# The query and output-weight products of an attention layer, made in two column halves of the array

## The chip, the cores and the metric

The kernel runs on one core of one Trainium2 chip. The metric is device time in microseconds (us) of one execution; three executions of the kernel before gave 2745.74, 2745.95 and 2746.96 us, and the median, 2745.95 us, is the time before.

## The reference

Four graph layers run over 4096 nodes with 256 features. Each ends in a residual sum and a row normalization. Layer 0 is the one that the change touches; layer 1 is a graph attention, layers 2 and 3 are products with the normalized adjacency matrix.

```
qkv = x @ Wqkv + bqkv                       # x: 4096 x 256, q, k, v: 256 wide each, 4 heads of 64
scores = einsum('hnd,hmd->hnm', q, k) * 64 ** -0.5
scores = scores + graph_bias * adj
scores = where(adj == 0, -1e9, scores)
attn = softmax(scores)
out = einsum('hnm,hmd->hnd', attn, v)       # heads side by side: 4096 x 256
x = layernorm(x + out @ Wout + bout)
```

Everything is in float32.

## The kernel before, in words

**Tiling of layer 0.** The 4096 rows are taken in 32 blocks of 128 (`Rows`, one for each block `ib`). A block has two pairs of heads (`Pair`, `pr` 0 and 1), and each pair goes through the 4096 columns in four steps of 1024. So one block is eight steps, and layer 0 is 256 steps, numbered `t`, with a tail of eight more. The keys (`kT`, in the tensor `store`) and the values (`v_sb`, in the tensor `xc`) stay on chip.

**A step.** `step(t)` writes the order of the work out by hand, under a manual schedule, as a software pipeline. On PE the order in a step is: `score` of the newest step (line 371), the transposes of the exponentials of head 0 of an older step (`turn`, line 410), `attend` of a step older still (line 428), then `finish` or `begin` if one is due, then the transposes of head 1 (line 410 again). ACT takes the exponentials (line 396), copies the transposed tiles out of PSUM (line 418) and makes the 0/1 edge mask with its row sums (line 295). DVE adds the bias and takes the maximum (line 380), makes the bias of the next block (lines 278, 283, 284) and does the small work of a pair. No planner is involved: what stands earlier in `step` is issued earlier on its engine.

**Which part of the array each product uses.** The page's forms tell it, as rows times columns:

- `score`: 64*128. Two heads of 64 features each stand in the two row halves.
- `turn`: 64*128. The two row halves of a tile are transposed by two instructions.
- `attend`: 128*64. `v_sb[:, ci, h * HD : (h + 1) * HD]` of one head (64 columns) is the stationary operand, and the head `j` of the pair writes the partitions `j * HD` to `(j + 1) * HD` of `po`. So the two heads stand in the two column halves.
- `begin` (query product, line 319) and `finish` (output-weight product, line 340): 128*128, the whole array.

A float32 product of the program appears as two MATMUL records with a weight load (LDWEIGHTS) each; a transpose appears as one. `attend` has 16 products and 32 records in a step, `begin` 4 products and 8 records, `finish` 2 products and 4 records.

**begin.** `Rows.begin` (lines 314 to 335) makes the queries of the next block from `wq_sb` and `self.xq` into the PSUM tile `pq`, in one bank of the two that `po` alternates between; DVE adds the query bias, scales, and writes `qT` (line 327). It is called once for a block, in its sixth step, right after `attend` and ahead of the second `turn`. The first two blocks are different: `begin` of block 0 lies in the preamble between two key projections (line 212), and that of block 1 lies between two `turn`s, because no `attend` runs yet.

**finish.** `Rows.finish` (lines 337 to 353) multiplies the scaled heads `oT` with `wout_sb` into the PSUM tile `pp`; DVE adds the residual (line 350), takes the statistics for the normalization (lines 115, 116), and SP writes the row block to DRAM. It is called once for a block, in the eighth step, right after `attend` and ahead of the second `turn`. The last one runs in the tail, after the product of line 609 and ahead of line 139.

Of the kernel before, what the change touches and what calls it, by code (L numbers as in the profile page):

```python
# [16 lines left out]
P = 128  # L17
N = 4096
D = 256
H = 4  # L20
HD = D // H
# [23 lines left out]
def tile_gnn(  # L45
# [18 lines left out]
    nc = tc.nc  # L64
# [48 lines left out]
    def ln_stats(pool, row, ci):  # L113
        st = pool.tile([P, 6], F32, tag="bnst", name="bnst")
        nc.vector.bn_stats(st, row)
        nc.vector.bn_aggr(mv[:, ci, :], st)
# [54 lines left out]
    with ExitStack() as l0:  # L171
# [16 lines left out]
        wq_sb = w_sb[:, :, 0:D]  # L188
# [3 lines left out]
        wout_sb = big.tile([P, 2, D], F32, name="wout_sb")  # L192
# [55 lines left out]
        class Rows:  # L248
# [65 lines left out]
            def begin(self, tag):  # L314
                self.qT = wk2.tile([P, 2, P], F32, tag="qT", name="qT")
                pq = ps_o.tile([P, 512], F32, tag=tag, name="pq")
                for pr in range(2):
                    for cc in range(2):
                        nc.tensor.matmul(  # L319
                            pq[:, pr * P : (pr + 1) * P],  # L320
                            wq_sb[:, cc, pr * P : (pr + 1) * P],
                            self.xq[:, cc, :],
                            start=(cc == 0),
                            stop=(cc == 1),
                        )
                for pr in range(2):
                    nc.vector.tensor_scalar(
                        self.qT[:, pr, :],
                        pq[:, pr * P : (pr + 1) * P],
                        bqk_sb[:, pr : pr + 1],  # L330
                        HD ** -0.5,
                        ALU.add,
                        ALU.mult,
                    )
                nc.gpsimd.tensor_tensor(self.xr, self.xr, bout_b, ALU.add)

            def finish(self, tag):
                pp = ps_o.tile([P, 512], F32, tag=tag, name="pp")
                for pr in range(2):
                    nc.tensor.matmul(  # L340
                        pp[:, 0:D],
                        self.oT[:, pr, :],
                        wout_sb[:, pr, :],
                        start=(pr == 0),
                        stop=(pr == 1),
                    )
                nc.vector.tensor_reduce(
                    rowsum[:, self.ib : self.ib + 1], self.rs, AX.X, ALU.add
                )
                nc.vector.tensor_tensor(self.xr, pp[:, 0:D], self.xr, ALU.add)  # L350
                ln_stats(wk2, self.xr, self.ib)
                if self.ib + 1 < NCH:
                    nc.sync.dma_start(x0_pre[self.ib * P : (self.ib + 1) * P, :], self.xr)
# [798 lines left out]
```

## Time and profile before

| what | value |
|---|---|
| median of three executions | 2745.95 us |
| profiled execution, its own time | 2743.03 us |
| profiled execution, span from the first to the last instruction | 2741.3 us |
| mean granted TensorE clock of the span | 0.993 |
| PE busy | 2688.6 us, 98% of the span |
| DVE busy | 2183.8 us, 80% |
| ACT busy | 1648.0 us, 60% |
| layer 0, first score to last score | about 20 us to 1355 us |

How to read it. PE is TensorE's matmuls, PEld its weight loads, DVE is VectorE, ACT is ScalarE, POOL is GpSimd, SP issues transfers. A matmul's record begins when it starts and ends when its last result is out, so records overlap; the distance between two starts tells what an instruction costs in a full stream, and its own duration is longer. A form such as `128*64 128x128` gives the rows and columns of the array in use, and then the size of the output or input. `<-` in a group stands between what is written and what is read. An "idle before" with "issue" as the releaser is time in which the engine waited for nothing that the profile shows.

### The profile page before, as it was taken

The page shows a single profiled execution, that of the slowest core. Times are in us where ns is not written, and L with a number is a line of the kernel's source. Part 1 is how long each engine was busy: PE and PEld are TensorE (multiplying, and loading weights), DVE is VectorE, ACT ScalarE, POOL GpSimd, SP SyncE. Part 2 cuts the span into 40 slices and gives each one's busy share as a digit, 9 for nine tenths or more (in the row PEclk, how much of TensorE's full clock was granted, in tenths as well). Part 3 has the DMA queues.
Part 4 walks back from the last instruction along what each step waited for, and adds up shares of the span by engine and source line. Part 5 has one row for each costly group of instructions (what it writes and reads, how often), then busy time and mean ns, then how long its engine had stood idle before and what let it go on. Part 6 is the DMA issues. An engine that isn't in the chain of part 4 may idle for free.

```text
span 2741.3 us, 58184 instructions
## 1 busy us (share of the span) xinstructions
PE 2688.6 (98%) x23440; PEld 1840.8 (67%) x23440; DVE 2183.8 (80%) x3995; ACT 1648.0 (60%) x2675; POOL 379.4 (14%) x660
## 2 busy tenths in 40 slices
PE   8999999999999999999979999999999999999997
PEld 5777777777777777777768888886444444444443
DVE  4899889899898989889758888885866578666565
ACT  2899999999999999999857777771100001000000
POOL 1232222232222222222200000001200000000000
PEclk9999999999999999999999999999999999999998
DMA  6444444444444444444352222203545544555552
GB/s 148 94 94 95 89 92 95 90 92 92 91 95 91 91 94 95 86 95 95 125 171 77 77 77 77 73 28 118 178 158 164 167 160 154 169 173 165 184 170 75
DMA packets 679486, 312.31 MB, mean 114 GB/s; under 512 B 553520, under 2 KB 583600, under 8 KB 679216
## 3 DMA queue, kind: packets, MB, share of 16 engines
q1 hardware_dynamic: 655776, 265.10, 38.9%
q0 software_dynamic: 21632, 42.05, 4.3%
q8 instruction: 183, 3.00, 0.5%
q10 hardware_dynamic: 1808, 1.44, 0.2%
q14 instruction: 87, 0.71, 0.1%
HBM read 262.41 MB, written 46.07 MB: 113 GB/s over the span
## 4 chain that ended last, share of the span: by engine, by line
PE 96%; DVE 2%; issue 1%; DMA 1%; ACT 1%; SPq 0%; POOL 0%; DVEq 0%; ACTq 0%; POOLq 0%
PE m L980 27%; PE po L428 18%; PE sc L371 16%; PE po L802 16%; PE ptr L410 11%; PE py L1014 2%; PE pp L340 1%; PE pq L319 1%; PE pv L232 1%; PE pk L212 1%; PE sc L139 1%; DMA xt<-in_xT 0%; SPq L262 0%; DMA rb<-norm 0%; DVE pt L416 0%
## 5 line engine op out<-in xcount | busy, mean ns | idle before, releaser
L380 DVE CUSTOM_DVE_ANT_0 z<-sc,bias 128x1024 f32<-128x1024 f32 x512 | 606.0, 1221 | 48.0 <-PE sc L371 47.9
L396 ACT ACTIVATE z<-z,nm 128x1024 f32<-128x1024 f32 x512 | 590.4, 1153 | 0.0
L418 ACT COPY pt<-ptr 128x1024 f32<-128x1024 f32 x507 | 510.5, 1007 | 78.3 <-PE ptr L410 75.2
L428 PE MATMUL po<-pt,xc 128*64 128x128 f32 x8192 | 504.1, 276 | 0.0
L371 PE MATMUL sc<-store,qT 64*128 64x512 f32 x2048 | 502.9, 604 | 0.1
L802 PE MATMUL po<-store,pt 128*128 128x257 f32 x2048 | 447.6, 380 | 12.6 <-issue 12.6
L428 PEld LDWEIGHTS po<-pt,xc 128*64 128x64 f32 x8192 | 442.1, 137 | 17.5 <-DVE pt L416 0.2
L410 PEld LDWEIGHTS ptr<-ident,z 64*128 64x128 f32 x8192 | 322.0, 138 | 178.4 <-issue 82.5
L802 PEld LDWEIGHTS po<-store,pt 128*128 128x128 f32 x2048 | 388.9, 190 | 71.1 <-issue 12.7
L980 PE MATMUL m<-asum,ysum 128*128 128x512 f32 x768 | 356.2, 593 | 6.3 <-issue 6.3
L410 PE MATMUL ptr<-ident,z 64*128 64x64 f32 x8192 | 356.6, 225 | 4.5 <-ACT pt L418 3.2
L371 PEld LDWEIGHTS sc<-store,qT 64*128 64x128 f32 x2048 | 192.7, 188 | 116.7 <-issue 109.8
L980 PEld LDWEIGHTS m<-asum,ysum 128*128 128x128 f32 x768 | 146.0, 190 | 177.9 <-issue 161.2
L980 PE MATMUL m<-asum,store 128*128 128x512 f32 x512 | 262.3, 594 | 0.0
L980 PE MATMUL m<-a,ysum 128*128 128x512 f32 x512 | 245.7, 593 | 0.0
L986 ACT COPY e<-m 128x512 f32<-128x512 f32 x32 | 18.5, 585 | 351.4 <-PE m L980 351.4
L301 POOL DMA_DIRECT2D edge<-mk x256 | 143.5, 561 | 558.7 <-ACT mk L295 544.7
L756 ACT ACTIVATE z<-z,es_q 128x1024 f32<-128x1024 f32 x128 | 146.5, 1145 | 120.8 <-DVE mx L743 114.4
L949 DVE TENSOR_TENSOR asum<-a 128x512 f32<-128x512 f32 x128 | 88.0, 688 | 164.1 <-PE m L980 164.1
L284 DVE SCALAR_TENSOR_TENSOR bias<-rt,gb,u 128x512 f32<-128x512 f32 x256 | 194.4, 759 | 9.1
L792 DVE STREAM_TRANSPOSE pt<-z 128x1024 f32<-128x1024 f32 x128 | 158.1, 1237 | 42.1 <-PE po L802 42.1
L278 DVE STREAM_TRANSPOSE rt<-raw 128x512 f32<-128x512 f32 x256 | 179.9, 703 | 0.3 <-issue 0.3
(122 smaller groups left out, 2528.8 us busy)
## 6 DMA issues: line engine op xcount, KB each, us to landing
a<-in_adjT SPq DMA_DIRECT2D x256, 512.0 KB, 5.2
raw<-in_adjT SPq DMA_DIRECT2D x512, 128.0 KB, 3.9
edge<-mk POOLq DMA_DIRECT2D x256, 128.0 KB, 2.3
mk<-edge SPq DMA_DIRECT2D x256, 128.0 KB, 2.9
xt<-in_xT SPq DMA_DIRECT2D x8, 512.0 KB, 4.6
xq<-in_xT SPq DMA_DIRECT2D x32, 128.0 KB, 3.9
xr<-in_x SPq DMA_DIRECT2D x32, 128.0 KB, 3.3
rb<-norm POOLq DMA_DIRECT2D x128, 32.0 KB, 2.4
```

The source lines that it names most:

```text
L278: nc.vector.transpose(rt.rearrange("p (b r) -> p b r", r=QB), self.raw_now[:, half * nb : (half + 1) * nb, :],)
L284: nc.vector.scalar_tensor_tensor(self.bias[k][:, m0 : m0 + HT], rt, gb, u, ALU.mult, ALU.add)
L371: nc.tensor.matmul(ps[j][:, q * 512 : (q + 1) * 512], self.rows.qT[j * HD : (j + 1) * HD, self.pr, :], kT[j * HD : (j + 1) * HD, self.pr, ...
L380: nc.vector.tensor_tensor_reduce(z, ps[j], self.rows.bias[k], 1.0, NEG, ALU.add, ALU.max, self.mx[:, j, k : k + 1],)
L396: nc.scalar.activation(z, z, AF.Exp, bias=self.nm[:, j : j + 1], accum_out=self.ls[:, j, k : k + 1],)
L410: nc.tensor.transpose(pa[:, r, c, :], z[half, c * P : (c + 1) * P], ident[half, half])
L418: nc.scalar.copy(to, pa)
L428: nc.tensor.matmul(self.po[j * HD : (j + 1) * HD, 0:P], v_sb[:, ci, h * HD : (h + 1) * HD], self.pt[j][k][:, c, :], start=(ci == 0), stop= ...
L756: nc.scalar.activation(self.z[s], self.z[s], AF.Prelu, bias=self.eq[:, s : s + 1], alpha=SLOPE)
L792: nc.vector.transpose(self.pt[:, :, s, :], self.z[s].rearrange("p (b r) -> p b r", r=QB))
L802: nc.tensor.matmul(self.po[:, 0 : D + 1], self.pt[:, b, :, :].rearrange("p s i -> p (s i)"), wh[:, b, :], start=(b == 0), stop=(b == NBK - 1),
L980: nc.tensor.matmul(self.m[i], left, right, start=(c == 0), stop=(c == NP - 1))
```

## The change

In `begin`, each of the four products of 128 stationary columns becomes two of 64 columns: head `j` of the pair writes partitions 0 to 63 or 64 to 127 of the same columns of `pq`. In `finish`, each of the two products does the same with 64 of the 128 rows of the block: the stationary operand is 64 columns of `oT`, and the output goes to one half of the partitions of `pp`. The moving operand of both halves is the same: `self.xq[:, cc, :]` (128 columns) in `begin`, `wout_sb[:, pr, :]` (256 columns) in `finish`. The sums are the same; so are the tiles, the transfers, the order on every engine, and everything that DVE does with the results.

```diff
@@ -316,13 +316,15 @@
                 pq = ps_o.tile([P, 512], F32, tag=tag, name="pq")
                 for pr in range(2):
                     for cc in range(2):
-                        nc.tensor.matmul(
-                            pq[:, pr * P : (pr + 1) * P],
-                            wq_sb[:, cc, pr * P : (pr + 1) * P],
-                            self.xq[:, cc, :],
-                            start=(cc == 0),
-                            stop=(cc == 1),
-                        )
+                        for j in range(2):
+                            h = 2 * pr + j
+                            nc.tensor.matmul(
+                                pq[j * HD : (j + 1) * HD, pr * P : (pr + 1) * P],
+                                wq_sb[:, cc, h * HD : (h + 1) * HD],
+                                self.xq[:, cc, :],
+                                start=(cc == 0),
+                                stop=(cc == 1),
+                            )
@@ -337,13 +339,14 @@
             def finish(self, tag):
                 pp = ps_o.tile([P, 512], F32, tag=tag, name="pp")
                 for pr in range(2):
-                    nc.tensor.matmul(
-                        pp[:, 0:D],
-                        self.oT[:, pr, :],
-                        wout_sb[:, pr, :],
-                        start=(pr == 0),
-                        stop=(pr == 1),
-                    )
+                    for j in range(2):
+                        nc.tensor.matmul(
+                            pp[j * HD : (j + 1) * HD, 0:D],
+                            self.oT[:, pr, j * HD : (j + 1) * HD],
+                            wout_sb[:, pr, :],
+                            start=(pr == 0),
+                            stop=(pr == 1),
+                        )
```

## The prediction

> **What bounds the kernel now.** I read the page's busy times and its chain of waits first.
>
> ```profile
> PE 2688.6 (98%) x23440; PEld 1840.8 (67%) x23440; DVE 2183.8 (80%) x3995; ACT 1648.0 (60%) x2675; POOL 379.4 (14%) x660
> PE 96%; DVE 2%; issue 1%; DMA 1%; ACT 1%; SPq 0%; POOL 0%; DVEq 0%; ACTq 0%; POOLq 0%
> ```
>
> PE is busy for 98% of the span and 96% of the chain that ended last is PE. These are averages, so I went to the stage that the change touches: busy time by engine over the eight steps of one row block (window, its length, then PE, PEld, DVE, ACT, POOL).
>
> ```profile
> 694.56:699.37 4.81, 4.81 (x73) 3.57 (x73) 4.63 (x8) 3.89 (x5) 2.71 (x5) 1.00 0.59 121
> 699.37:705.23 5.86, 5.86 (x78) 4.23 (x76) 4.85 (x12) 5.83 (x12) 0.55 (x1) 1.00 0.33 74
> 705.23:710.04 4.81, 4.81 (x74) 3.56 (x73) 4.49 (x9) 3.88 (x5) 0.54 (x1) 1.00 0.49 109
> 710.04:715.00 4.96, 4.96 (x75) 4.25 (x74) 4.82 (x11) 4.81 (x9) 2.75 (x5) 1.00 0.43 83
> 715.00:719.80 4.80, 4.80 (x74) 3.55 (x73) 4.46 (x8) 4.80 (x9) 0.60 (x2) 1.00 0.64 123
> 719.80:724.60 4.80, 4.80 (x74) 3.56 (x72) 4.38 (x9) 4.80 (x9) 0.55 (x1) 1.00 0.48 114
> 724.60:729.41 4.81, 4.81 (x75) 3.57 (x74) 4.34 (x9) 4.81 (x9) 0.54 (x1) 1.00 0.50 97
> 729.41:735.30 5.89, 5.89 (x83) 4.53 (x81) 4.75 (x12) 5.83 (x12) 3.57 (x6) 1.00 0.35 72
> ```
>
> PE fills every step. The reader is to see two things: the steps with `finish` (5.86) and `begin` (5.89) are 1.06 and 1.09 us longer than a plain one (4.80), and DVE and ACT are close behind PE in all of them, so I have to ask whether they let a shorter PE through. The order on PE, from the timeline (start, length of the records, engine, line):
>
> ```profile
> 693.47 1.16 PE L319 MATMUL pq<-xq,w_sb 128*128 128x128 f32 x8
> 694.56 0.71 PE L410 MATMUL ptr<-ident,z 64*128 64x64 f32 x16
> ...
> 697.47 1.97 PE L428 MATMUL po<-pt,xc 128*64 128x128 f32 x32
> 699.37 0.71 PE L410 MATMUL ptr<-ident,z 64*128 64x64 f32 x16
> ...
> 702.27 1.97 PE L428 MATMUL po<-pt,xc 128*64 128x128 f32 x32
> 704.17 1.13 PE L340 MATMUL pp<-wout_sb,oT 128*128 128x256 f32 x4
> 705.23 0.71 PE L410 MATMUL ptr<-ident,z 64*128 64x64 f32 x16
> ```
>
> From start to next start: `pq` takes 694.56 - 693.47 = 1.09 us for 8 records, `pp` 705.23 - 704.17 = 1.06 us for 4, and `attend` 1.90 us for 32. An `attend` record with 128 moving columns thus costs less than half of a `pq` record with as many.
>
> Where the time inside goes I read from the starts of the single instructions in the trace; the figures are medians of the distance from one start to the next. `attend`: the two column halves start 6 ns apart and the next pair 103 ns later, so **a pair costs 109 ns**; the first pair costs 160. `pq`: 112 ns a record, the first 213. `pp`: 216 a record, the first 320. Across a change of line: `attend` to `turn` 203, to `pq` 203, to `pp` 202; `pq` to `turn` 206; `pp` to `turn` 310. A normal successor would have started after 103, 112 and 216. So **each change of the array's division costs 94 to 100 ns**, and then the first record of a 128-column load another 101 to 104, that of `attend`'s 64-column load 51.
>
> A control in the same trace: where the key projections (line 212) pass to the value projections (line 232), both on the whole array, the first value record comes 429 ns later (the usual distance of a 512-column record) and lasts 379 ns; where it follows a `score` in two row halves it lasts 483. And `turn` to `score`, both 64*128, takes 58 ns, the distance inside `turn`. It is the change of division that costs, not the change of line.
>
> **What the Trainium skill says.** TensorEngine Tiling (Array Packing), Key Properties: "Changing tiling mode (not just tile) drains the TensorE", and different tiles can load and multiply in parallel. The trace agrees on both: 94 to 100 ns at each change, none without one, and 6 ns between `attend`'s halves. TensorE: Matmul & The Clock Gate, LDWEIGHTS (loading the stationary operand): the load takes the number of columns over 1.2 in ns, 53 for 64 columns and 107 for 128. The exposed first loads of 51 and 101 to 104 ns fit; the transposes do not (their loads, recorded as 64x128, expose only some 48). PSUM — Partial Sum Buffer, on bank collisions: different column tiles may write one bank at once on disjoint partitions; `po` is written so, at 109 ns a pair, and `pq` and `pp` would be.
>
> **The change part by part.**
>
> *begin.* Removed: 8 full-array records, the change of division ahead of them and the first load; with 1.09 us to the next start, `pq` inserted between `attend` and `turn` costs 203 + 1089 - 203 = 1089 ns. Added: 16 records in 8 pairs, of exactly `attend`'s form (128*64, 128 moving columns). They follow `attend` without a change of division, and the change to `turn` that comes after them is the one `attend` pays anyway. So 8 x 109 = 872 ns. Saved: **217 ns**. Of this about 97 is the drain, 101 the first load, the rest 3 ns a product.
>
> *finish.* Removed: 202 + 1062 - 203 = 1061 ns. Added: 4 pairs with 256 moving columns. No row shows that form. Nearest from above and below: two row halves with 512 columns take 5 + 424 = 429 ns a pair (`score`), the whole array with 256 columns 216 a record. Both are 0.84 ns a column, so I take 216 for a pair and 4 x 216 = 864. Saved: **197 ns**. The bounds of a pair: 213, since a 128-column pair at 109 cannot be beaten by more than its 2 or 3 ns of fixed cost, and 432 if the halves ran one after the other (a rival below).
>
> *How often.* 30 times `begin` and 31 times `finish` lie between `attend` and `turn`: 30 x 0.217 = 6.5, 31 x 0.197 = 6.1, together **12.6 us**.
>
> *The rest.* `begin` of block 0 lies between two full-array projections. It gains two changes and a 128-column first load on the way back, about 0.3 us; PE waits 0.8 ahead of it and 0.2 behind it, so less is left. `begin` of block 1 lies between `turn`s and saves only the shorter first load and 3 ns a product, 0.07 us. The last `finish` saves some 0.05 us on its result and gives a change and a load, 0.2 us, to line 139 behind it. I set these three at nothing, with -0.1 to 0.5 us as bounds. The added 24 records and 24 loads of a block need no queue but PE's; no transfer, wait or tile is added or moved.
>
> *Does it reach the end?* While PE does `pq`, DVE waits for it; the same with `pp`, and ACT waits for the `turn` behind each:
>
> ```profile
> 694.67 0.61 DVE L327 TENSOR_SCALAR qT<-pq,bqk_sb 128x128 f32<-128x128 f32 x2 [1.10 <-PE pq L319]
> 695.31 1.01 ACT L418 COPY pt<-ptr 128x1024 f32<-128x1024 f32 x1 [0.81 <-PE ptr L410]
> 705.41 0.42 DVE L350 TENSOR_TENSOR xr<-pp,xr 128x256 f32<-128x256 f32 x1 [0.88 <-PE pp L340]
> 705.99 1.01 ACT L418 COPY pt<-ptr 128x1024 f32<-128x1024 f32 x1 [0.78 <-PE ptr L410]
> ```
>
> These four stand idle for 1.10, 0.81, 0.88 and 0.78 us just there (the brackets). Taking 0.2 us from PE shortens these waits and uncovers nothing, and what waits is released at the same distance from the following `turn`: the last record of `pq` ends 0.07 us after `turn`'s start now (206 ns to the next start, 275 long), and a last half, like `attend`'s, would too (203 and 273). So I let the whole 12.6 us through. One stall, the 0.16 us by which the fourth window (4.96) exceeds 4.80, comes from DVE: two steps after `finish` the second head's scores start 0.16 us after the first's, waiting for its PSUM tile. DVE is late from the work behind `pp`, keeps its distance to PE, and so I expect the stall unchanged.
>
> **The sum.** The profiled execution took 2743.03 us, its span 2741.3 and 1.7 around it; less 12.6 that is 2730.4. The median of the runs shown lies 2.9 above the profiled one, so for a median 2745.95 - 12.6 = 2733.35, say **2733.4 us**, 0.46% less.
>
> **The rivals.**
>
> *The halves run one after the other* (slower). In `attend` the two halves have moving operands of their own; in the change both read the same one, `xq` or `wout_sb`. No row of the trace shows two column halves that share their moving operand. If reading it twice kept the halves apart, `begin` would cost 16 x 109 = 1744 ns against 1089 now, `finish` 8 x 216 = 1728 against 1061: +0.655 x 30 + 0.667 x 31 = +40 us, 2786 us. It decides from a pair of 136 ns (1089 / 8) in `begin` and 265 (1061 / 4) in `finish`; below these the change gains. Against it: the operands of `attend`'s halves come from the same partitions too, and 6 ns between starts shows that two streams from one partition fit. I give it 0.07.
>
> *Another engine becomes the bound* (gain lost). For it: ACT's busy time is 4.80 of 4.80 us in the plain steps. Against it: ACT idles 0.8 us in each long step, four times what is taken, and over the block DVE has 36.7 and ACT 38.7 of 40.7 us, against 0.41 saved. If it took half the gain, 2739.6 us; all of it, 2746. I give it 0.08, half of that within 0.2% of before.
>
> *The changes of division stay* (the edit doesn't save what I think). If PE drained at the change of source or bank and not of division, each insertion would keep about 98 for the drain and 51 for the first load: 872 + 149 = 1021 against 1089, 864 + 149 = 1013 against 1061; 30 x 0.068 + 31 x 0.048 = 3.5 us, 2742.4, within what counts as the same. The two controls above speak against it. I give it 0.07.
>
> **How the numbers follow.** The forecast has 0.78. Its own range is 2730 to 2737: the spread of the runs shown (-0.2, +1.0), the bounds above, and up to 1.7 us from the granted clock, which in this trace stands at half for 17 us and 7 us about the passages between layers and may change phase when layer 0 ends earlier. Reaching up to 2740 takes in half a gain lost and leaves some 2 in 10 out. A difference of 0.2%, 5.5 us, is about what a measurement of this kernel can tell from no change. Faster by more: 0.78 and half of the second rival, 0.82. The same: the third rival and the rest of the second, 0.11. Slower: 0.07.
>
> **What would show it.** Right: in the trace after, 203 ns at most once between `attend` and `turn`; 103 ns from the last `attend` record to the first of `pq` and of `pp`; pairs of 109 and 216 ns; the windows of `finish` and `begin` at 5.66 and 5.67 us, all others as they are; DVE's wait for `pq` down from 1.10 to about 0.9. Wrong: pairs over 136 and 265 ns (the halves don't overlap), 203 ns ahead of `pq` (the drain stays), or plain steps longer than 4.80 us (another engine holds PE back).

## The result and the profile after

The changed kernel takes **2733.18 us** (median of 6 runs, 2731.42 to 2734.35), against 2745.6 us before (6 runs, 2742.57 to 2746.96); the ratio is 0.9959 (95% interval 0.9947 to 0.997). That is 12.4 us less, where 12.6 was forecast.

First come two lines of the page after: busy times, and the chain by engine.

```profile
PE 2677.8 (98%) x23824; PEld 1836.4 (67%) x23824; DVE 2183.5 (80%) x3995; ACT 1647.8 (60%) x2675; POOL 379.4 (14%) x660
PE 94%; DVE 2%; DMA 2%; issue 1%; ACT 1%; SPq 0%; POOL 0%; DVEq 0%; POOLq 0%; ACTq 0%
```

PE has 384 records more, and 10.8 us less of busy time; the other engines do what they did. PE is still the bound. Lines from 319 on have moved: `pq` is line 321 now, `pp` 343, `attend` 431, `score` 374, `turn` 413. Six of the eight steps of one row block after (window, length, PE, PEld, DVE, ACT, POOL):

```profile
689.04:693.85 4.81, 4.81 (x75) 3.58 (x74) 4.62 (x8) 4.05 (x7) 3.43 (x6) 1.00 0.51 112
693.85:699.51 5.66, 5.66 (x82) 4.06 (x81) 4.73 (x12) 5.66 (x12) 0.54 (x1) 1.00 0.41 87
699.51:704.32 4.81, 4.81 (x76) 3.57 (x74) 4.48 (x9) 4.06 (x7) 0.54 (x1) 1.00 0.49 109
704.32:709.29 4.97, 4.97 (x75) 4.30 (x74) 4.83 (x11) 4.81 (x9) 2.80 (x5) 1.00 0.44 82
709.29:714.09 4.80, 4.80 (x75) 3.56 (x74) 4.46 (x8) 4.79 (x9) 0.55 (x1) 1.00 0.62 120
...
723.71:729.38 5.67, 5.67 (x90) 4.43 (x89) 4.75 (x12) 5.67 (x12) 3.19 (x6) 1.00 0.28 59
```

The step of `finish` takes 5.66 us where it took 5.86, the step of `begin` 5.67 where it took 5.89. The plain steps are the same to 0.01 us, and the fourth window still has its stall (4.97). The order on PE, from the timeline (start, length of the records), first around `finish`, then around `begin`:

```profile
698.55 1.03 PE L343 MATMUL pp<-wout_sb,oT 128*64 128x256 f32 x8
699.51 0.71 PE L413 MATMUL ptr<-ident,z 64*128 64x64 f32 x15
...
726.61 1.97 PE L431 MATMUL po<-pt,xc 128*64 128x128 f32 x32
728.41 1.04 PE L321 MATMUL pq<-xq,w_sb 128*64 128x128 f32 x16
729.38 0.71 PE L413 MATMUL ptr<-ident,z 64*128 64x64 f32 x16
```

`attend` gives way to `pq` after 728.41 - 726.61 = 1.80 us and not 1.90: its last pair is followed as any other pair is. `pq` takes 0.97 us for 16 records where it took 1.09 for 8, and `pp` 0.96 us for 8 where it took 1.06 for 4. The form column says 128*64 for `pq` and `pp`; it was 128*128.

From the starts of the single instructions (medians of 30 or 31 places):

| distance, ns | before | after |
|---|---|---|
| last record of `attend` to `pq` | 203 | 103 |
| `pq`: first record or pair, then each | 213, 112 | 109, 109 |
| last record of `pq` to `turn` | 206 | 204 |
| last record of `attend` to `pp` | 202 | 104 |
| `pp`: first record or pair, then each | 320, 216 | 216, 216 |
| last record of `pp` to `turn` | 310 | 310 |

The profiled execution alone took 2734.35 us, only 8.7 less than the 2743.03 of before, though layer 0 from first to last score fell by 12.0 us (1332.85 to 1320.83). Two differences elsewhere take part of this back. The first score starts 1.0 us later, waiting for a transfer, and layers 2 and 3 take 3.0 us longer (851.0 against 848.1), with 25.0 us at half the granted clock against 18.6. These two lengths go together in all twelve profiles of this case: layers 2 and 3 take 847.8 to 848.5 us with 18.3 to 19.1 us at half clock, and 850.3 to 851.1 us with 20.9 to 25.0. A second profile of the changed kernel, below, is of the first kind (847.8 us with 18.3 at half clock) and took 2733.05.

### The profile page after: what moved, and what is told of

Its sections match the earlier page's. It is cut to its first block, busy times and chain, and to the rows that moved or that the text cites. A ratio compares the mean times of both kernels' runs of the same rounds, so it can differ in the third digit from the quotient of the medians.

```text
span 2732.6 us, 58953 instructions
## 1 busy us (share of the span) xinstructions
PE 2677.8 (98%) x23824; PEld 1836.4 (67%) x23824; DVE 2183.5 (80%) x3995; ACT 1647.8 (60%) x2675; POOL 379.4 (14%) x660
## 4 chain that ended last, share of the span: by engine, by line
PE 94%; DVE 2%; DMA 2%; issue 1%; ACT 1%; SPq 0%; POOL 0%; DVEq 0%; POOLq 0%; ACTq 0%
PE m L983 28%; PE po L431 17%; PE sc L374 16%; PE po L805 16%; PE ptr L413 11%; PE py L1017 2%; PE pp L343 1%; PE pq L321 1%; PE pv L232 1%; PE pk L212 1%; DMA xt<-in_xT 0%; DMA mk<-edge 0%; DMA norm<-lt 0%; DMA x<-xs 0%; SPq L731 0%
## 5 line engine op out<-in xcount | busy, mean ns | idle before, releaser
L805 PE MATMUL po<-store,pt 128*128 128x257 f32 x2048 | 447.2, 380 | 12.6 <-issue 12.6
L983 PEld LDWEIGHTS m<-asum,store 128*128 128x128 f32 x512 | 97.9, 191 | 123.2 <-issue 121.3
```

Of the source, the lines that this page charges most:

```text
L805: nc.tensor.matmul(self.po[:, 0 : D + 1], self.pt[:, b, :, :].rearrange("p s i -> p (s i)"), wh[:, b, :], start=(b == 0), stop=(b == NBK - 1),
L983: nc.tensor.matmul(self.m[i], left, right, start=(c == 0), stop=(c == NP - 1))
```

## The experiments

All times are medians; beside each stands the kernel before, measured together with it on the same chip.

| run | time, us | before beside it | ratio to before (95% interval) | step of begin / finish, us |
|---|---|---|---|---|
| the change | 2733.18 | 2745.6 | 0.9959 (0.9947 to 0.997) | 5.68 / 5.67 |
| the change again | 2734.34 | 2744.77 | 0.9962 (0.9949 to 0.9976) | 5.68 / 5.67 |
| begin alone | 2739.29 | 2746.24 | 0.9977 (0.9968 to 0.9986) | 5.68 / 5.87 |
| finish alone | 2740.99 | 2746.24 | 0.998 (0.9972 to 0.9987) | 5.89 / 5.67 |
| four quarters | 2743.28 | 2746.24 | 0.9994 (0.9986 to 1.0002) | 5.82 / 5.80 |
| one half after the other | 2749.59 | 2746.24 | 1.0011 (1.0004 to 1.0018) | 6.16 / 5.72 |
| begin after the second turn, halves | 2742.78 | 2744.92 | 0.9991 (0.9983 to 0.9999) | 5.92 / 5.67 |
| begin after the second turn, whole | 2746.23 | 2744.92 | 1.0003 (0.9995 to 1.0012) | 5.99 / 5.67 |
| results after the bias | 2729.2 | 2744.92 | 0.994 (0.9927 to 0.9952) | 5.68 / 5.67 |
| halves by fours in begin | 2738.53 (one run) | 2744.77 | none | 5.73 / 5.67 |
| results after the bias, first begin whole | 2728.99 | 2746.34 | 0.9934 (0.992 to 0.9949) | 5.68 / 5.67 |

The steps in the last column are medians over all row blocks of layer 0 but the first three and the last, from `score` to `score`; in the kernel before they are 5.89 and 5.86. They tell more than the times, which differ from run to run by some microseconds, part of it with the half clock.

### One part at a time

Each of these two runs keeps one of the two hunks of the change. Expected of begin alone:

> Only begin is made in column halves; finish stays on the whole array. Theory (each inserted product saves the change of division ahead of it and its exposed first load): begin costs 872 ns between attend and turn, finish stays at 1061, so 30 x 0.217 = 6.5 us less than before, about 2739.1 us. Rival (one of the two carries the whole gain, or a second one gives nothing once the first has made room for DVE and ACT): 12.4 us less, or nothing.

and of finish alone:

> Only finish is made in column halves; begin stays on the whole array. Theory: finish costs 864 ns, begin stays at 1089, so 31 x 0.197 = 6.1 us less than before, about 2739.5 us; together with the run of begin alone it adds up to the gain of the change. Rival: the two gains don't add up.

Measured: 7.0 and 5.3 us less than before, 12.2 together, against 12.4 for the change. In each run the step of the product that was made in halves is that of the change, and the other is that of before. The two gains add up; neither needs the other, and DVE and ACT let both through.

### The same place, another division

Here both products are made in four quarters of 32 columns. The excerpt shows `begin` in short form; `finish` is altered in the same way.

```diff
-for j in range(2):
-    pq[j * HD : (j + 1) * HD, ...], wq_sb[:, cc, h * HD : (h + 1) * HD]
+for j in range(NA):                                 # 4 quarters of QB = 32 columns
+    pq[j * QB : (j + 1) * QB, ...], wq_sb[:, cc, pr * P + j * QB : pr * P + (j + 1) * QB]
```

> Both products are made in four column quarters (128*32) and not in attend's halves, so the array's division changes ahead of them again, while four small products overlap instead of two. Theory (what counts is that the division stays that of attend): 203 ns from the last attend record to pq and pp again, a first load exposed for 25 to 50 ns, then about 112 and 216 ns for four quarters; some 0.15 us more for each begin and 0.14 for each finish than in halves, 2742 us. Rival (what counts is that small products overlap their weight loads): no slower than in halves, 2733 us or less.

```profile
733.09 1.97 PE L431 MATMUL po<-pt,xc 128*64 128x128 f32 x32
734.99 1.08 PE L321 MATMUL pq<-xq,w_sb 128*32 128x128 f32 x32
736.00 0.71 PE L413 MATMUL ptr<-ident,z 64*128 64x64 f32 x16
```

In this timeline of the kernel with quarters `attend` takes 1.90 us to the next start again: with a form of 128*32 behind it, the cost of the change of division is back. The single starts give 202 ns from `attend` to `pq` and 203 to `pp`, a first group 24 ns longer than the others (113 against 89 to the next group), and 110 ns for four quarters, about as much as two halves take. The steps are 0.138 and 0.135 us longer than the change's; 0.15 and 0.14 were expected, and nothing by the rival. So the division that stays `attend`'s is worth the larger part. The smaller part is the first load, which is shorter when it is narrower.

### The same division, another place

In these two runs `begin` moves behind the second `turn`, so that it stands between two products in row halves. It is made in halves in one run and on the whole array in the other; `finish` stays in halves in both.

```diff
-                if pr == 1 and k == NS - 3:
-                    rows[ib + 1].begin(tag_o if attends else "po1")
...
             if turns:
                 pairs[ut].turn(kt, 1, by_dve=not live)
+            if grow and pr == 1 and k == NS - 3:
+                rows[ib + 1].begin(tag_o if attends else "po1")
```

> The changed kernel with begin moved on PE to stand between the second turn and the next score, both in row halves; DVE takes its result after the bias of the next block. begin and finish are in column halves. Theory (the gain is the change of division that attend and begin share): begin now needs a change on either side and a first load of 64 columns, 152 - 58 + 1026 = 1120 ns instead of 872, 30 x 0.25 = 7.4 us more than the change, 2740.6 us. Rival (halves are cheaper by themselves): as the change, 2733 us.

> As the run with begin between turn and score, but begin on the whole array; finish in column halves. Theory: begin costs 152 + 1089 - 58 = 1183 ns there, only 63 more than in halves at the same place, 30 x 0.063 = 1.9 us; about 2742.5 us. Rival (halves are cheaper by themselves): 0.217 us more for each begin than in halves at the same place, 6.5 us.

The kernel with halves in that place, from its timeline:

```profile
733.45 0.71 PE L413 MATMUL ptr<-ident,z 64*128 64x64 f32 x16
734.10 1.09 PE L321 MATMUL pq<-xq,w_sb 128*64 128x128 f32 x16
735.12 1.99 PE L374 MATMUL sc<-store,qT 64*128 64x512 f32 x8
```

`turn` to the next start takes 0.65 us, where it takes 0.54 ahead of a `score` (723.85 to 724.39 in the same kernel), and the `pq` of the same form and count takes 1.02 us instead of 0.97. The step is 0.246 us longer than the change's, where the theory has 0.25; on the whole array it is another 0.064 longer, as the theory's 0.063, and not 0.217. **So halves by themselves are worth 64 ns; the other 150 of the gain come from the neighbour.** The whole block of eight steps is 0.30 us longer and not 0.25: the sum had left out that the `score` behind `begin` now has its first load exposed for longer (533 ns to its second pair after `pq`, 485 after `turn`), and so the step after begin takes 4.86 us. The times alone would not have decided: the two runs lie 3.5 us apart, between the 1.9 of the theory and the 6.5 of the rival, and the profile of the second has 48 us at half clock against 38. That DVE takes the result of `begin` later in both does not lengthen the steps: a run below alters only the order on DVE, and they stay at 5.68 and 5.67 us.

### One half after the other

```diff
-for pr in range(2):
-    for cc in range(2):
-        for j in range(2):
+for j in range(2):
+    for pr in range(2):
+        for cc in range(2):
```

and the same in `finish` (`j` outside, `pr` inside).

> The halves of the change, in another order of the loops: first everything for the lower half, then everything for the upper half. The division is that of attend all the same. Theory (two products overlap only when they follow each other in different halves): 112 ns for each of 16 records in begin and 216 for each of 8 in finish, so 1.79 and 1.73 us instead of 0.87 and 0.86, and 30 x 0.92 + 31 x 0.86 = 54 us more than the change, 2788 us. Rival (PE looks ahead far enough to overlap halves in any order): 2733 us.

Neither held. The step of `begin` grew by 0.49 us and that of `finish` by only 0.05. From the kernel's timeline:

```profile
736.72 1.53 PE L321 MATMUL pq<-xq,w_sb 128*64 128x128 f32 x16
738.18 0.71 PE L413 MATMUL ptr<-ident,z 64*128 64x64 f32 x16
...
747.69 1.08 PE L343 MATMUL pp<-wout_sb,oT 128*64 128x256 f32 x8
748.71 0.71 PE L413 MATMUL ptr<-ident,z 64*128 64x64 f32 x16
```

`pq` takes 1.46 us to the next start, half again as much as in the change; `pp` takes 1.02 against 0.96. The distances between the starts in `pq` are 109, 109, 109, 109, 6, 103, 57, 53, 57, 53, 57, 109, 109, 109, 109 ns. The trace doesn't name the half of a record. But records of one half follow each other after 109 ns and not after 6, so this reads as four records of the lower half alone, then, from the fifth on, the two halves together, then the rest of the upper half alone. The compiled program has eight records of the lower half ahead of the first of the upper. That one started 6 ns after the fifth, so it overtook three; it stands four places behind the fifth. In `pp`, with four records a half, the first of the upper half starts 6 ns after the very first record: again four places. So there is a new theory: PE starts a record of a free half as soon as a record up to four places ahead of it starts in the other half.

To test it, the order was changed in `begin` alone: `for pr`, `for j`, `for cc`, so that four records of one half and four of the other take turns.

> The changed kernel with one order changed in begin: for each pair of heads first the four records of the lower half, then the four of the upper, and so on; finish as in the change. The run that made one half after the other showed a record of the upper half starting 6 ns after one of the lower half that was four records ahead of it in the program. Theory (PE starts a record of the free half up to four records ahead of its turn): halves overlap almost fully again, begin costs some 50 ns more than in the change, as finish did in that run, and its step takes 5.73 us. Rival (records start in the order of the program, and the earlier run's order was another one): only neighbours of different halves overlap, 13 x 109 + 203 ns from the first record to the next turn, a step of 6.2 us.

```profile
731.26 1.09 PE L321 MATMUL pq<-xq,w_sb 128*64 128x128 f32 x16
732.28 0.71 PE L413 MATMUL ptr<-ident,z 64*128 64x64 f32 x16
```

Measured: 1.02 us from `pq` to `turn` and a step of begin of 5.73 us, with distances of 6, 103, 57, 52, 57, 53 ns and so on: the halves run together from the first record. That is the theory's 5.73 and not the rival's 6.2. That the reach is four places and no more rests on the earlier run alone, where the first record of the upper half did not start with the fourth, five places ahead of it.

### The stall that was left

This is the changed kernel with the order on DVE altered: `begin` and `finish` are split, and their DVE part is issued behind `make_bias`. The excerpt shows the order in `step`.

```diff
                     begun.begin(tag_o if attends else "po1")      # PE part and the sum on POOL
...
                 rows[ib + 1].make_bias(kb, half)
...
+            if begun:
+                begun.begin_dve()
+            if done:
+                done.finish_dve()
```

> The changed kernel with the same order on PE; DVE takes the results of begin and finish after it has made the bias of the next block, and not ahead of it. Theory (the 0.16 us stall of the scores, two steps after finish, comes from DVE, which stands waiting for pp with the bias behind it): the waits of 0.89 us for pq and 0.70 us for pp go, and so does the stall, 31 x 0.165 = 5 us less than the change, 2728 us. Rival (DVE's total work or ACT sets that stall): 2733 us. Third: the later release of the PSUM bank holds attend back, over 2733 us.

In the changed kernel DVE waits for `pp` with the whole bias behind it:

```profile
699.70 0.42 DVE L353 TENSOR_TENSOR xr<-pp,xr 128x256 f32<-128x256 f32 x1 [0.70 <-PE pp L343]
700.16 0.43 DVE L115 BATCH_NORM_STATS2 bnst<-xr 128x6 f32<-128x256 f32 x1
700.62 0.18 DVE L116 BATCH_NORM_AGGREGATE mv<-bnst 128x2 f32<-128x6 f32 x1
700.72 0.68 DVE L278 STREAM_TRANSPOSE rt<-raw 128x512 f32<-128x512 f32 x1
```

With the order altered the bias comes first, `pp` is long there when DVE gets to it, and no wait is left in the line:

```profile
696.83 0.70 DVE L278 STREAM_TRANSPOSE rt<-raw 128x512 f32<-128x512 f32 x1
697.57 0.43 DVE L283 TENSOR_SCALAR u<-rt 128x512 f32<-128x512 f32 x1
698.03 0.75 DVE L284 SCALAR_TENSOR_TENSOR bias<-rt,gb,u 128x512 f32<-128x512 f32 x1
698.70 0.15 DVE L358 TENSOR_REDUCE rowsum<-rs 128x1 f32<-128x8 f32 x1
698.77 0.42 DVE L361 TENSOR_TENSOR xr<-pp,xr 128x256 f32<-128x256 f32 x1
```

and the step that had the stall is a plain one in the altered kernel:

```profile
702.30:707.10 4.80, 4.80 (x74) 3.56 (x72) 4.66 (x11) 4.80 (x9) 2.71 (x5) 1.00 0.51 96
```

The median of that step falls from 4.97 to 4.80 us, layer 0 from 1320.83 to 1315.20, and the time to 2729.2 us, 0.994 of before. That is faster than the kernel before. Against the change the intervals of the two ratios still overlap a little (up to 0.9952 here, from 0.9947 there), and it is the 5.6 us of layer 0 that show the gain. The stall was a wait in DVE's queue and not DVE's total work, which did not shrink (2188.0 us busy against 2183.5). The run moves both results; which of the two waits made the stall was not tried one by one.

### The first begin, and the change again

In the profiles seen so far, the first score started at 20.2 to 20.7 us where the first `begin` was whole (three kernels), and at 21.1 and later where it was in halves or quarters. The next run is the kernel of the last section with `if self.ib == 0` choosing the whole array in `begin`:

> The run with the results taken after the bias, and in it only the first begin, which lies between two whole-array projections, made on the whole array again. In the profiles of kernels whose first begin is whole the first score starts at 20.2 to 20.7 us, in those with halves at 21.1 us and later. Theory (halves in that place cost it): the first score comes back to 20.2 to 20.7, and the time is 0.5 us lower, too little for the rounds to tell. Rival (chance of the first transfers): 21.1 us or later as before. Layer 0 behind it is unchanged in both.

```profile
14.64 1.13 PE L320 MATMUL pq<-xq,w_sb 128*128 128x128 f32 x8 [1.44 <-DMA xq<-in_xT]
17.78 5.40 PE L212 MATMUL pk<-xt,wkv_sb 128*128 128x512 f32 x8 [2.01 <-DMA xt<-in_xT]
23.11 1.99 PE L391 MATMUL sc<-store,qT 64*128 64x512 f32 x8
```

The whole-array `begin` is done, and the key projection behind it still waits 2.01 us for its input and starts at 17.78, later than in the change (17.53). The score starts at 23.1 us, later still because that projection took 5.40 us and not 3.70: the granted clock stood at half from 18.0 to 21.4 us. The rival holds: in this execution the place is set by the transfer of `xt`, not by how the product is made. 2728.99 us is not distinguishable from the run without this edit.

The change itself, once more:

> The changed kernel unaltered, on another chip, for the comparison with the runs that change it or do one part: the steps of begin and finish 5.68 and 5.67 us, layer 0 as in the first profile of the change, and a median 12.5 us below before if the gain is layer 0's alone; the rest of the difference between single executions follows how long the granted clock stands at half.

The two steps take 5.68 and 5.67 us. Layer 0 takes 1321.88 us, 1.05 more than in the first profile, with 3.4 us at half clock near its end. The time is 10.4 us less than the runs of before beside it (ratio 0.9962). Its interval reaches from 6.6 to 14 us, and the expected 12.5 lies in it.

## Why the prediction was right

*The bound.* PE filled every step before and fills it after. All of the time that left PE left the steps; no plain step grew by more than 0.01 us.

*begin.* Forecast 217 ns a block, measured 5.892 - 5.677 = 0.215 us. Its parts are 100 ns at the way in (203 to 103), 101 of the first load (213 to 112 or 109), and for the rest 3 ns a record. The runs behind `turn` show 150 of it to depend on the neighbour: without it only the shorter first load (51 instead of 101) and the 3 ns a record remain.

*finish.* Forecast 197 ns, measured 0.195 to 0.197 us. The form that no row showed, column halves with 256 moving columns, costs 216 ns a pair, the value taken from two rows with the same time a column.

*The drain and the first load.* That a change of the array's division drains PE (the Trainium skill, TensorEngine Tiling (Array Packing), Key Properties) agrees with the runs as far as its cost goes: quarters, which change the division, pay 100 ns at the very place where halves don't. Whether the array empties is not shown: by the trace the last record of `attend`, 273 ns long, has 70 ns still to run when a product of another division starts 203 ns after it. The exposed first load went with the columns loaded, as the Trainium skill has it (TensorE: Matmul & The Clock Gate, LDWEIGHTS (loading the stationary operand)): 24 ns for 32 columns, 51 for 64, 101 for 128, close to 27, 53 and 107, the estimates that its formula gives.

*The cover.* DVE's wait for `pq` fell from 1.10 to 0.90 us, its wait for `pp` from 0.88 to 0.70:

```profile
689.16 0.61 DVE L329 TENSOR_SCALAR qT<-pq,bqk_sb 128x128 f32<-128x128 f32 x2 [0.90 <-PE pq L321]
```

One reading was inexact: by the windows, ACT does not idle in the long steps (5.83 us busy) but at the head of the windows behind them, 3.89 and 3.88 us busy before, 4.05 and 4.06 after. The cover was there all the same. The stall stayed, and grew by 0.01 us (4.961 to 4.972 in the median), which is 0.3 us in all; the sum had nothing for it.

*What was set at nothing.* The first `begin` doesn't show: it is hidden behind a transfer, as the run with the first `begin` whole tells. From the start of the last `finish` to the line behind it takes 1014 ns where it took 938, too little for the times to show. The allowance for the granted clock was too small for single executions: the one with 6.4 us more at half clock in layers 2 and 3 took 3.0 us longer there, more than the 1.7 allowed.

*The rivals.* The halves do overlap though they read one moving operand: 109 and 216 ns a pair, with 6 ns between starts. Another engine did not become the bound. The changes of division did not stay.

*What was luck.* The steps bear the forecast out: 30 x 0.215 + 31 x 0.196 = 12.5 us, less 0.3 for the stall. That the median fell within 0.2 us of the forecast is luck: the six runs of the change lie up to 2.9 us apart, and the second measurement gave 10.4 us instead of 12.4.

## What to carry to other kernels

Where PE is the bound, look at the form column from one product to the next. A small product between two large ones should use the same division of the array as the one ahead of it, even if it needs twice the instructions, and it should stand where it shares a change that is paid anyway. Here each change of division cost 94 to 100 ns and exposed a first load of 24 to 101 ns, while halves between two changes gained only 64 ns over the whole array. An equal division spares the change but not always the first load: `score` behind `turn`, both 64*128, still takes 485 ns to its second pair and 429 from pair to pair, before and after.

And where DVE takes a small product's result, put work that doesn't need it ahead of the wait; here that was worth 5.6 us of layer 0.

## What the runs showed of the hardware that was not expected

PE does not start its records strictly in the order of the program when they go to different halves of the array: a record of the free half started 6 ns after one four places ahead of it, past three of the other half. The change itself makes use of this, and so does `attend`: a product's two records are neighbours in the compiled program, so two of the lower half come ahead of two of the upper, and yet the starts are 6 and 103 ns apart in turn. So halves need not alternate record by record; in groups of four they cost only 50 ns more for a `begin`, while in groups of eight they cost 490 ns.
